# Scan stage of a vision-Mamba kernel on one core: dut tiles issued three products ahead, C rows before B rows, y stores in sub-slots 1 and 3, a third y buffer

## The chip, the core and the metric

The kernel runs on one core of one Trainium2 chip. The metric is the device time of one launch in microseconds (us). A core has five engines that run side by side, each with its own instruction stream: PE (TensorE, matrix products), DVE (VectorE), ACT (ScalarE), POOL (GpSimd) and SP (SyncE). SP computes nothing: here it issues every DMA, in the order of its stream. "HBM" is the chip's main memory; SBUF and PSUM are the core's own memories.

## What is computed

The reference takes x of shape 8 x 96 x 64 x 64 and runs two layers: a state-space block, then attention without softmax and a quantised feed-forward block. The part that matters here is the selective scan of the first layer. For each image, each of four directions k, each of 192 channels and each of 16 states, along L = 4096 positions:

```python
def step(h, t):
    u_t, d_t, B_t, C_t = t
    dA = jnp.exp(d_t[..., None] * A)
    h = dA * h + (d_t * u_t)[..., None] * B_t[:, :, None, :]
    y = jnp.einsum('bkdn,bkn->bkd', h, C_t)
    return (h, y)
```

So a decay factor dA, a driving term delta*u*B, a linear recurrence over time, and a sum over the 16 states weighted by C.

## The kernel before

Eight images are handled as four pairs. For each pair the kernel first prepares delta, delta*u, B and C in scratch buffers in HBM (`dl`, `du`, `bs`, `cs`), then calls `scan` (L442). The preparation of a pair overlaps the closing stages of the pair before; `scan` runs alone. All times of `scan` below come four times in a launch.

`scan` walks over 128 steps: four directions, and in each 32 chunks of TC = 128 positions. Directions 2 and 3 run backwards. A chunk is cut into four quarters r of six channel groups, and each quarter into two halves z. The step loop (L656) has eight sub-slots v = 0..7 in a step, and p = 8s + v counts them over the whole scan. The schedule is written out by hand (`manual_schedule`, L444): every engine executes its instructions in the order in which the loop emits them, and only semaphores let one engine wait for another.

What the loop emits, with the engine that does it:

- `decay(p + 2)` (L572): six PE products of `aw` and `dm` into one of three PSUM buffers `da`, then an exponential on ACT (L588). It is two sub-slots ahead of its use.
- `drive(p // 2 + 2)` (L545), in even sub-slots: the driving term of one quarter. ACT copies the state at the end of the chunk before into the start column (L560; POOL's memset L558 at a direction's start), and POOL multiplies `dut` (delta*u) by the B rows of `bc` into `dbu` (L563). `dbu` has three buffers. One such POOL instruction is called a product below, and products are numbered g = 4s + r.
- `run(p)` (L590): the recurrence, one DVE instruction (L599) on a half of a quarter. It reads `da` from PSUM and `dbu` from SBUF and writes `h`. Two runs use one product.
- `sums(s - 1, f)` (L604): the sum over states of the step before, small PE products of `h` and `cw` (L617), and twice in a step an ACT evacuation into the y buffer `yev` (L625), at f = 3 (sub-slot v = 2) and f = 7 (v = 6).
- `fetch(g)` (L529): SP's load of `dut[g]`, 384 KB, into one of five buffers. The load of tile g must wait until product g - 5 has read the same buffer. Before the change, sub-slot p emits `fetch(p // 2 + 4)` after `drive(p // 2 + 2)`, thus two products ahead.
- `load(s + 2, v // 2)` (L478), in odd sub-slots: two SP loads of `dm` (L489, L490), 144 and 48 KB, for the decay two steps later.
- `load_aw` (L470): the weights of the next direction, four loads of 384 KB, only in a direction's last step.
- `load_bc(s + 2)` (L492): B rows and C rows for two chunks (NB = 2), as four SP loads of 128 KB (L501), one after each of the sub-slots v = 0..3 of an even step. Before the change the two B loads come first, the two C loads second.
- `diagonal(s + 1)` (L509): from the C rows, the weights `cw` for the sums. It is spread over the eight sub-slots of an odd step; each has one ACT instruction (L517), which reads the C rows in `bc`, and one SP load of 16 KB (L523).
- `store(s - 2, j)` (L630): SP's store of one half of `yev`, 96 KB (L635). Before the change in v = 2 and v = 6, from one of two `yev` buffers.

The order on SP's stream within a sub-slot is thus: `fetch` or `load` (and `load_aw`), then `store`, then the one load of `load_bc` or `diagonal`. In two steps, one even and one odd, SP issues 8 dut, 16 dm, 4 bc, 8 cw and 4 y transfers, 40 in all.

Of the kernel before, what the change touches and what calls it, by code (L numbers as in the profile page):

```python
# [10 lines left out]
F32 = mybir.dt.float32  # L11
# [26 lines left out]
HQ = TC // 4  # L38
NE = 24
# [13 lines left out]
def vss_attn_ffn(ctx: ExitStack, tc: tile.TileContext, a: dict):  # L53
# [388 lines left out]
    def scan(dl, du, bs, cs_, ys):  # L442
        with ExitStack() as st:
# [4 lines left out]
            wk = st.enter_context(tc.tile_pool(name="s2", bufs=2))  # L448
            trio = st.enter_context(tc.tile_pool(name="s3", bufs=3))
# [18 lines left out]
            aw, dm, bc, dut, dbu, hs, yev = {}, {}, {}, {}, {}, {}, {}  # L468

            def load_aw(k, r):  # L470

                aw[k, r] = one.tile([128, NI, 2, 128], BF16, name=f"aw{r}")
                w = 2 * NI * 128
                nc.sync.dma_start(
                    aw[k, r].rearrange("p i z m -> p (i z m)"), awd[k, :, r * w : r * w + w]
                )
# [15 lines left out]
            def load_bc(s):  # L492

                if s >= N:
                    return
                k, c, _ = steps[s]
                i = s // NB
                bc[i] = wk.tile([128, 2, 2, NB * TC], F32, name="bc")
                for w, v in enumerate((bs, cs_)):
                    for b in range(2):  # L500
                        nc.sync.dma_start(  # L501
                            bc[i][64 * b : 64 * b + 64, w].rearrange("p z t -> p (z t)"),
                            v[k, c // NB, 16 * b : 16 * b + 16]
                            .rearrange("(n z) t -> n (z t)", z=2)
                            .unsqueeze(0).to_broadcast([8, 8, 2 * NB * TC]),
                        )
                        yield
# [21 lines left out]
            def fetch(g):  # L529

                if g >= 4 * N:
                    return
                k, c, _ = steps[g // 4]
                o = NI * (g % 4)
                dut[g] = quad.tile([128, NI, TC], F32, name="dut")
                nc.sync.dma_start(
                    dut[g].rearrange("p i t -> p (i t)"),
                    du[k, c, :, o : o + NI].rearrange("m i t -> m (i t)").unsqueeze(1)
                    .to_broadcast([16, 8, NI * TC]),
                )  # L540
# [4 lines left out]
            def drive(g):  # L545

                if g >= 4 * N:
                    return
                s, r = divmod(g, 4)
                k, c, first = steps[s]  # L550
                back = k >= 2
                t = trio.tile([128, 2 * W6 + 1], F32, name="dbu")
                if back:
                    start = t[:, 1:].rearrange("p (z i u) -> p z i u", z=2, u=SEG)[:, :, :, TC]
                else:
                    start = segs(t)[:, :, :, 0]
                if first:
                    nc.gpsimd.memset(start, 0.0)  # L558
                else:
                    nc.scalar.copy(  # L560
                        start, segs(hs[s - 1][:, :, r])[:, :, :, 1 if back else TC]
                    )
                nc.gpsimd.tensor_tensor(  # L563
                    segs(t)[:, :, :, 1:],
                    dut[g].unsqueeze(1)
                    .to_broadcast([128, 2, NI, TC]),
                    bc[s // NB][:, 0, :, bass.ts(c % NB, TC)].unsqueeze(2)
                    .to_broadcast([128, 2, NI, TC]), ALU.mult,
                )
                dbu[g] = t  # L570

            def decay(p):  # L572

                if p >= 8 * N:
                    return
                s, v = divmod(p, 8)
                r, z = divmod(v, 2)
                k, c, _ = steps[s]
                e = da[p % 3][:, 0:W6].rearrange("p (i u) -> p i u", u=SEG)[:, :, 1:]
                for i in range(NI):  # L580
                    nc.tensor.matmul(  # L581
                        e[:, i], aw[k, r][:, i, z, :], dm[s // 2][:, NI * r + i, bass.ts(c % 2, TC)],
                        start=True, stop=True,
                    )
                if p == 0:
                    table("ln", lambda: nc.scalar.activation(e, e, AF.Exp))
                else:
                    nc.scalar.activation(e, e, AF.Exp)  # L588

            def run(p):  # L590
                s, v = divmod(p, 8)
                r, z = divmod(v, 2)
                if v == 0:
                    hs[s] = wk.tile([128, 2 * W6 + 1, NR], F32, name="h")
                o = 1 if steps[s][0] >= 2 else 0
                d = slice(None, None, -1) if o else slice(None)

                w = slice(z * W6 + o, z * W6 + o + W6)
                nc.vector.tensor_tensor_scan(  # L599
                    hs[s][:, w, r][:, d], da[p % 3][:, o : o + W6][:, d],  # L600
                    dbu[4 * s + r][:, w][:, d], 0.0, ALU.mult, ALU.add,
                )

            def sums(s, f):  # L604


                c = steps[s][1]
                if f == 0:
                    yev[s] = wk.tile([128, 2, HQ // 2, NE], F32, name="yev")
                y = yp[f // 4]  # L610
                h = hs[s][:, 1:, :].rearrange("p (z i u) r -> p z i u r", z=2, u=SEG)
                w = cw[s // NB % 2][:, :, c % NB].rearrange("p z m (j t) -> p z (m j) t", j=2)
                for i in range(2 * (f % 4), 2 * (f % 4) + 2):
                    for z in range(2):
                        for q in range(4):
                            t = 16 * q + 8 * (f // 4) + i
                            nc.tensor.matmul(  # L617
                                y[32 * q : 32 * q + 32, 2 * NE * i : 2 * NE * i + 2 * NE]
                                .rearrange("p (j r i) -> p i j r", j=2, r=NR),
                                w[:, z, :, t], h[:, z, :, t : TC : TC // 2, :],  # L620
                                start=(i + z == 0), stop=(i + z == 8),
                            )
                if f % 4 == 3:
                    o = 8 * (f // 4)
                    nc.scalar.activation(  # L625
                        yev[s][:, :, o : o + 8, :].rearrange("p j i e -> p i j e"),
                        y[:, 0 : 16 * NE].rearrange("p (i j e) -> p i j e", j=2, e=NE), AF.Copy,
                    )

            def store(s, j):  # L630
                k, c, _ = steps[s]
                v = ys[k, :, c * TC : (c + 1) * TC, :].rearrange(
                    "m (j q i) e -> j q m (i e)", j=2, q=4
                )
                nc.sync.dma_start(v[j], yev[s][j::2, j].rearrange("p i e -> p (i e)"))  # L635
# [6 lines left out]
            for _ in load_bc(0):  # L642
                pass
# [4 lines left out]
                pass  # L648
            fetch(2)
            fetch(3)  # L650
            more = iter(())
            drive(0)
            drive(1)
# [2 lines left out]
            for s in range(N + 2):  # L656
                for v in range(8):
                    p = 8 * s + v
                    if s < N:
                        decay(p + 2)  # L660
                        if v % 2 == 0:
                            drive(p // 2 + 2)
                        run(p)
                    if 0 < s <= N:
                        for f in ((0, 1), (2,), (3,), (4,), (5,), (6,), (7,), ())[v]:
                            sums(s - 1, f)
                    if s < N:
                        if v % 2 == 0:
                            fetch(p // 2 + 4)
                        else:  # L670
                            load(s + 2, v // 2)
                        if s + 1 < N and steps[s + 1][2] and v % 2 == 1:
                            load_aw(steps[s + 1][0], v // 2)
                    if v in (2, 6) and s > 1:
                        store(s - 2, v // 4)
                    if v == 0:
                        more = diagonal(s + 1) if s % NB else load_bc(s + NB)
                    next(more, None)
# [216 lines left out]
    for pair in range(npair + 1):  # L895
# [60 lines left out]
        if new:  # L956
            scan(new["dl"], new["du"], new["bs"], new["cs"], new["ys"])
# [115 lines left out]
```

## Time and profile before

| what | us |
|---|---|
| median of three launches | 11598.43 (11579.95 to 11607.51) |
| the profiled execution: its time | 11616.03 |
| the profiled execution: its span, first to last instruction | 11613.8 |
| scan of pair 0, stretch 597 to 2500 of the span | 1903: DVE busy 1759.1, POOL 1774.2, ACT 1266.5, PE 1289.7 |
| the other three scans, stretches cut alike | 1911, 1900, 1904 |
| DMA engines in the scan of pair 0 | mean busy share 0.75, 198 GB/s |
| mean granted TensorE clock | 0.818 of full speed |

The profile is one execution with the hardware profiler on. Its page has the busy time of each engine, 40 equal slices of the span, the DMA queues, the chain of work that ended last, the costliest groups of instructions and the DMA issues. Further views of the trace list waits, instructions in order of time, and busy time in chosen stretches. "SPq" marks instructions of SP's sequencer. A row "A <- B: t, n, m" in the view of waits means that A's engine stood idle t us in total, n times, at most m us, until B released it. The program's page does not count DMA-issuing instructions as busy, so SP has no busy share there; its load has to be read from the timeline.

### The profile page before, as it was taken

How to read it: one execution, taken by the hardware profiler on the slowest of the kernel's cores; microseconds unless marked ns; L12 is line 12 of the kernel's file. 1: busy time of each engine (PE TensorE's matmuls, PEld its weight loads, DVE VectorE, ACT ScalarE, POOL GpSimd, SP SyncE). 2: the span in 40 equal slices, each digit the busy share in tenths (PEclk: the TensorE clock that was granted, in tenths of full speed). 3: DMA queues.
4: the chain of work that ended last, by engine and by line, in shares of the span. 5: the costliest groups of instructions: out<-in, count | busy, mean ns of one | idle time of the engine just before them, and what ended most of it. 6: DMA issues, size and time to landing. Idle time of an engine off the chain costs nothing. (4 is left out here: it accounts for less than half of the span.)

```text
span 11613.8 us, 392166 instructions
## 1 busy us (share of the span) xinstructions
PE 8533.6 (73%) x170112; PEld 5690.3 (49%) x170112; DVE 8826.8 (76%) x6465; ACT 6941.0 (60%) x12227; POOL 7976.2 (69%) x2770
## 2 busy tenths in 40 slices
PE   7866666679876666667996666666898666666687
PEld 2255555544325555554422555555442355555542
DVE  5489999963659999995366999999445799999922
ACT  3666666644556666664455666666446566666623
POOL 0489999960259999994026999999203799999900
PEclk8778878889768787888977888888896787888886
DMA  2977777765477777776557777777636877777762
GB/s 83 234 196 203 199 201 201 200 169 137 131 198 198 200 197 202 204 200 157 123 150 204 198 202 198 201 205 198 150 98 180 206 199 201 202 199 202 194 137 62
DMA packets 1755459, 2096.48 MB, mean 181 GB/s; under 512 B 438019, under 2 KB 1340676, under 8 KB 1750916
## 3 DMA queue, kind: packets, MB, share of 16 engines
q1 hardware_dynamic: 1753732, 2071.39, 68.3%
q8 instruction: 1335, 21.87, 0.8%
q14 instruction: 392, 3.21, 0.1%
HBM read 1606.70 MB, written 464.01 MB: 178 GB/s over the span
## 5 line engine op out<-in xcount | busy, mean ns | idle before, releaser
L599 DVE TENSOR_TENSOR_SCAN h<-da,dbu 128x774 f32<-128x774 f32 x4096 | 7034.7, 1759 | 599.7 <-POOL dbu L563 450.3
L563 POOL TENSOR_TENSOR dbu<-dut,bc 128x1536 f32<-128x1536 f32 x2048 | 7092.1, 3509 | 546.5 <-DMA dut<-du 334.2
L581 PE MATMUL da<-dm,aw 128*128 128x128 bf16 x24576 | 2488.2, 250 | 2523.7 <-DVE h L599 2313.4
L588 ACT ACTIVATE da<-da 128x768 f32<-128x768 f32 x4092 | 3255.0, 796 | 1583.2 <-PE da L581 1572.2
L581 PEld LDWEIGHTS <-aw 128*128 128x128 bf16 x24576 | 1943.3, 111 | 2809.5 <-issue 2444.5
L617 PE MATMUL yp<-h,cw 128*32 128x48 f32 x131072 | 2995.4, 246 | 38.7 <-issue 25.3
L617 PEld LDWEIGHTS yp<-h,cw 128*32 128x32 f32 x131072 | 2475.2, 155 | 526.3 <-issue 257.2
L517 ACT ACTIVATE cw<-bc,blk 128x512 f32<-128x512 f32 x2048 | 1462.9, 716 | 574.8 <-DMA bc<-cs 492.6
L757 POOL TENSOR_TENSOR yk<-yk 128x768 f32<-128x768 f32 x64 | 116.5, 1820 | 1267.3 <-DMA yk<-ys 1095.3
L433 POOL TENSOR_TENSOR dp<-rest,dp 128x512 bf16<-128x512 f32 x384 | 473.8, 1237 | 680.6 <-ACT dp L432 678.8
L625 ACT ACTIVATE yev<-yp 128x384 f32<-128x384 f32 x1024 | 504.1, 492 | 466.5 <-DMA ys<-yev 336.0
L431 DVE TENSOR_TENSOR rest<-delta,dp 128x512 f32<-128x512 f32 x384 | 335.3, 876 | 426.9 <-ACT dp L430 426.6
L410 PE MATMUL pq<-S,dtw 12*128 12x512 f32 x768 | 555.5, 833 | 111.8 <-ACT delta L414 95.7
L798 DVE SCALAR_TENSOR_TENSOR g<-yc,c_onw,yrs 96x512 f32<-96x512 f32 x128 | 89.9, 742 | 473.3 <-ACT yrs L190 473.3
L870 POOL TENSOR_TENSOR ot<-t,y 96x512 f32<-96x512 f32 x64 | 101.8, 1591 | 487.8 <-DVE y L868 395.6
L560 ACT COPY dbu<-h 128x12 f32<-128x12 f32 x1984 | 404.0, 204 | 0.0
L432 ACT ACTIVATE dp<-rest 128x512 bf16<-128x512 f32 x384 | 240.1, 628 | 272.5 <-DVE rest L431 272.1
L410 PEld LDWEIGHTS pq<-S,dtw 12*128 12x128 f32 x768 | 154.6, 236 | 497.2 <-ACT delta L414 262.0
L684 ACT ACTIVATE nsq<-ncp 96x512 f32<-96x512 f32 x128 | 75.8, 592 | 533.2 <-PE ncp L682 506.5
L390 POOL COPY u<-xi 128x512 f32<-128x512 f32 x96 | 100.6, 1063 | 347.4 <-ACT xi L356 293.5
L770 PEld LDWEIGHTS py<-ident,yk 128*24 128x24 f32 x8192 | 228.2, 106 | 225.0 <-issue 169.1
L770 PE MATMUL py<-ident,yk 128*24 128x128 f32 x8192 | 310.2, 285 | 26.7 <-DVE yk L756 22.7
(136 smaller groups left out, 6783.5 us busy)
## 6 DMA issues: line engine op xcount, KB each, us to landing
dut<-du SPq DMA_DIRECT2D x2048, 384.0 KB
dm<-dl SPq DMA_DIRECT2D x2048, 144.0 KB
dl<-dp SPq DMA_DIRECT2D x256, 384.0 KB
dm<-dl SPq DMA_DIRECT2D x2048, 48.0 KB
ys<-yev SPq DMA_DIRECT2D x1024, 96.0 KB
du<-du SPq DMA_DIRECT2D x256, 256.0 KB
bc<-bs SPq DMA_DIRECT2D x512, 128.0 KB
bc<-cs SPq DMA_DIRECT2D x512, 128.0 KB
```

The costliest lines, as they stand in the source:

```text
L410: nc.tensor.matmul(pq, dtw[64:76, k, T], S[64:76], start=True, stop=True)
L431: nc.vector.tensor_tensor(rest, d, dp[:, :, 0], ALU.subtract)
L433: nc.gpsimd.tensor_tensor(dp[:, :, 2], rest, dp[:, :, 1], ALU.subtract)
L517: nc.scalar.activation(cw[i % 2][:, :, :, m, :].rearrange("p z j t -> p (z j) t"), bc[i][:, 1].rearrange("p z (j t) -> p (z j) t", j=NB), ...
L560: nc.scalar.copy(start, segs(hs[s - 1][:, :, r])[:, :, :, 1 if back else TC])
L563: nc.gpsimd.tensor_tensor(segs(t)[:, :, :, 1:], dut[g].unsqueeze(1) .to_broadcast([128, 2, NI, TC]), bc[s // NB][:, 0, :, bass.ts(c % NB, ...
L581: nc.tensor.matmul(e[:, i], aw[k, r][:, i, z, :], dm[s // 2][:, NI * r + i, bass.ts(c % 2, TC)], start=True, stop=True,)
L588: nc.scalar.activation(e, e, AF.Exp)
L599: nc.vector.tensor_tensor_scan(hs[s][:, w, r][:, d], da[p % 3][:, o : o + W6][:, d], dbu[4 * s + r][:, w][:, d], 0.0, ALU.mult, ALU.add,)
L617: nc.tensor.matmul(y[32 * q : 32 * q + 32, 2 * NE * i : 2 * NE * i + 2 * NE] .rearrange("p (j r i) -> p i j r", j=2, r=NR), w[:, z, :, t], ...
L625: nc.scalar.activation(yev[s][:, :, o : o + 8, :].rearrange("p j i e -> p i j e"), y[:, 0 : 16 * NE].rearrange("p (i j e) -> p i j e", j=2 ...
L770: nc.tensor.matmul(o, yk[:, k, 4 * g + e, NE * j : NE * j + NE], ident, start=False, stop=(k + j == 4),)
```

## The change

Four edits, all inside `scan`:

1. `load_bc` issues the two C loads first and the two B loads second.
2. `yev` moves from the pool with two buffers to the pool with three (one more tile of 3 KB in each partition).
3. `fetch(4)` is issued before the loop, and even sub-slots issue `fetch(p // 2 + 5)` in place of `fetch(p // 2 + 4)`. The tile then goes out three products ahead of the product that the same sub-slot emits. The number of `dut` buffers stays five.
4. The two stores of step s - 2 go out in sub-slots v = 0 and v = 2 of step s (the first and the third) in place of v = 2 and v = 6.

PE, DVE, ACT and POOL keep their instructions and their order. Only the order of SP's stream changes, and which buffers are shared.

```diff
@@ load_bc
-                for w, v in enumerate((bs, cs_)):
+                for w, v in ((1, cs_), (0, bs)):
                     for b in range(2):
                         nc.sync.dma_start(
@@ sums
                 if f == 0:
-                    yev[s] = wk.tile([128, 2, HQ // 2, NE], F32, name="yev")
+                    yev[s] = trio.tile([128, 2, HQ // 2, NE], F32, name="yev")
@@ before the loop
             fetch(2)
             fetch(3)
+            fetch(4)
@@ the loop
                         if v % 2 == 0:
-                            fetch(p // 2 + 4)
+                            fetch(p // 2 + 5)
                         else:
                             load(s + 2, v // 2)
...
-                    if v in (2, 6) and s > 1:
-                        store(s - 2, v // 4)
+                    if v in (0, 2) and s > 1:
+                        store(s - 2, v // 2)
```

In SP's stream of an even and an odd step, numbered from the even step's first `fetch`, the stores stand at places 6, 15, 24 and 35 before the change and at 1, 7, 19 and 25 after it; the C loads at 7 and 10 before and at 2 and 5 after; the B loads at 1 and 4 before and at 8 and 11 after.

## The prediction

> **What bounds the kernel now.** I read the page's costliest groups first. Each group line gives line, engine, operation and shapes, then busy us and mean ns, then idle us before it and what ended most of that idle.
>
> ```profile
> L599 DVE TENSOR_TENSOR_SCAN h<-da,dbu 128x774 f32<-128x774 f32 x4096 | 7034.7, 1759 | 599.7 <-POOL dbu L563 450.3
> L563 POOL TENSOR_TENSOR dbu<-dut,bc 128x1536 f32<-128x1536 f32 x2048 | 7092.1, 3509 | 546.5 <-DMA dut<-du 334.2
> ...
> L517 ACT ACTIVATE cw<-bc,blk 128x512 f32<-128x512 f32 x2048 | 1462.9, 716 | 574.8 <-DMA bc<-cs 492.6
> ...
> L625 ACT ACTIVATE yev<-yp 128x384 f32<-128x384 f32 x1024 | 504.1, 492 | 466.5 <-DMA ys<-yev 336.0
> ```
>
> The four scans are the long stages. DVE waits for POOL's product, POOL waits for dut, and ACT waits for C rows and for y stores. These are the waits that the four edits aim at. But a wait for a DMA can mean "issued too late in the order" or "the queue cannot go faster". So I read POOL's timeline next (start, length; 8 products are two chunks):
>
> ```profile
> 1306.66 27.70 POOL L563 TENSOR_TENSOR dbu<-dut,bc 128x1536 f32<-128x1536 f32 x8 [2.08 <-DMA dut<-du]
> 1335.95 27.71 POOL L563 TENSOR_TENSOR dbu<-dut,bc 128x1536 f32<-128x1536 f32 x8 [1.59 <-DMA dut<-du]
> ```
>
> POOL runs eight products without a gap in 27.70 us, then loses about 1.8 us, once in two chunks. Two chunks are also SP's cycle: one even chunk with four bc loads, one odd chunk with eight cw loads, 40 issues in all. The SP timeline from the end of an even chunk's first half:
>
> ```profile
> 1327.84 0.58 SPq L501 DMA_DIRECT2D bc<-cs  x1
> 1328.53 0.54 SPq L536 DMA_DIRECT2D dut<-du  x1
> 1329.48 0.58 SPq L489 DMA_DIRECT2D dm<-dl  x1
> 1330.69 0.31 SPq L490 DMA_DIRECT2D dm<-dl  x1
> 1331.69 0.52 SPq L536 DMA_DIRECT2D dut<-du  x1
> 1332.69 0.59 SPq L635 DMA_DIRECT2D ys<-yev  x1
> ...
> 1338.24 0.70 SPq L523 DMA_DIRECT2D cw<-cs  x1
> 1339.05 0.56 SPq L536 DMA_DIRECT2D dut<-du  x1
> 1339.70 0.64 SPq L635 DMA_DIRECT2D ys<-yev  x1
> 1340.39 0.68 SPq L523 DMA_DIRECT2D cw<-cs  x1
> ```
>
> SP issues back to back, 0.55 to 0.70 us each, except in a few holes around 1329 to 1333. The queue's own waits over the run say what those holes are:
>
> ```profile
> SPq L523 <- DMA dut<-du: 194.5, 273, 1.7
> SPq L635 <- DMA bc<-cs: 114.8, 197, 1.4
> SPq L490 <- DMA dut<-du: 104.5, 184, 1.5
> ```
>
> A cw load does not need a dut tile. In the built program each SP issue waits for the landing of the issue eight places before it (eight completion semaphores in turn), so at most eight transfers are in flight. Averaged over the steady part of the four scans, SP's cycle of 40 issues is 29.64 us: 24.65 in issues, 2.15 in hand-overs of 0.05 to 0.10 us, 2.69 waiting for the landing eight back, 0.16 other. The cycles without weight loads take 29.47. So SP is never idle for want of work, and it never waits for POOL: a dut issue stands 7 to 9 us after the product that freed its buffer. An early cycle of the first scan settles it: POOL still had a lead and took 27.68 us, while SP took 29.55. SP sets the pace; the others queue behind it.
>
> **What the Trainium skill says.** "DMA: Bandwidth & Descriptors", section "Why a DMA increments its semaphore by 16 and not by 1": a transfer uses the largest count of engines up to 16 that divides the slowest dimension of both sides, on this path the lowest-numbered ones, and the sequencer posts the rest of the count at once. The landing records agree: 16 engine landings for a dut or dm load, one early record and eight landings for a bc or cw load, one and four for a y store. So engines 0 to 3 carry everything, and 8 to 15 only dut and dm. Section "Queues, rings and completion order" of that page: an engine takes descriptors in ring order. This agrees: a y store issued after a dut in the crowded stretch lands 5.8 us after its issue, in a quiet stretch 4.1. "Perfetto Trace Analysis", section "DMA Instruction — HWDGE (DVE, Sync)": an issue's row ends when the sequencer is free, not when data landed; here the rows are 0.54 us and a dut lands 4.2 to 7.1 us after issue. "SBUF — State Buffer", section "Who interferes with whom": a DVE instruction with one SBUF input does not contend with GpSimd. The scan's other input is in PSUM, and 16 scans and 8 products lie side by side in 27.7 us each, so I price no collision.
>
> **The change part by part.** Number SP's issues in a cycle from 0, the even chunk's first dut.
>
> *Look-ahead of three.* No issue is added in the cycle; dut 4 goes out before the loop. Each dut stands 3.46 us (one product) earlier in the order, moved past one dm pair, one or two bc or cw loads and at times a store, which each go out one place (0.65 us) later and have slack of 8 slots and more. Its wait for product g-5 stays met: 7 to 9 us of slack minus 3.46 is over 3.5. This removes POOL's stall as seen against SP's order, but not SP's 29.47 us, so POOL's wait comes back later in the run. What remains is the end of each scan: the last dut stands one product nearer to the scan's first, worth up to 3.46 x 4 = 14 us, at least 0. I take 10.
>
> *C before B.* The same four bc transfers of 128 KB trade places: 0 on SP. ACT's wait for C (492.6/256 = 1.9 us a cycle) shrinks, but ACT is off the path: DVE waits little for it. B then lands about 13 us into the cycle, and its first reader runs at about 17 even with compute one product earlier, so this has cover. At a scan's start B lands some 3 us later and delays product 0, which the wait for the third dut (product 2 starts 20 us after the first issue) hides: 0.
>
> *Third y buffer.* ACT's 336.0 us wait for y stores goes. ACT has slack; nothing on SP: 0. If ACT were on the path, it would be worth up to 336.
>
> *Stores in sub-slots 1 and 3.* A store needs an evacuation two slots back, long done. All four stores stay, but stand at issues 1, 7, 19, 25 instead of 6, 15, 24, 35. This moves the landings that SP waits for, and is the only edit that can move SP's cycle. Averages of the trace: SP waits only from issue 12 to 24. The wait that decides is the one of issue 23, at 17.79 us, for the landing of issue 15, at 17.44. Issues 0 to 15 are the same sixteen transfers in both orders (4 dut, 4 bc, 2 y, 3 pairs of dm). If engines 0 to 3 work without a pause, that landing does not move. Today they pause early: issues 1, 2, 3 land 0.91, 0.82 and 0.48 us apart, against 1.1, 0.55 and 0.29 later for bc and the two dm, so the dm gaps hold about 0.5 us of idle. A store at issue 1 fills this: gain 0 to 0.5, I take 0.3. After issue 23 seventeen issues remain in both, with one store (0.66) less and one cw (0.73) more: +0.07. Stores at 19 and 25 make issue 27 wait for landing 19. Reckoned from the landing steps (dm 0.55 and 0.25, dut 1.1, y 0.77), landing 19 comes 0.45 us before issue 27 is due, so only the scatter of cycles (28.36 to 30.77 us, 5th to 95th percentile) makes it wait: 0 to 0.5, I take 0.1. Sum -0.3 + 0.07 + 0.1 = -0.13 us a cycle, bounds -0.43 to +0.57. Over 256 cycles: -33 us, bounds -110 to +146.
>
> Sum: -33 - 10 = -43 us against the profiled execution's 11616.03, so 11573. That execution is 17.6 above the median of 11598.43, so **11555**.
>
> **Rivals.** (1) *The order is the fault, not the queue.* With all waits gone POOL would run 27.70 a cycle: 256 x (29.47 - 27.70) = 453 us less, about 11145. For it: POOL's 334.2 us on dut, ACT's 828.6. Against: SP's 24.65 + 2.15 + 2.85, of which only the 2.85 can go. (2) *Nothing moves.* The landings of the same bytes decide, and all is within 0.2%: about 11590. (3) *Slower: the stores crowd engines 0 to 3.* A store right behind the dut at the start of both chunks, beside C or cw loads, and an even second half of only dut and dm, where eight issues hold more bytes. If this keeps SP waiting past issue 27, each y landing (0.77) that falls into the binding stretch counts: at +0.4 a cycle 102 - 10 = +92, so 11690. It decides the sign once SP's waits rise by over 0.04 us a cycle (10/256).
>
> **How the numbers follow.** A measurement of this kernel can tell about 0.2% (23 us) from no change. Chances: the small gain 0.45, around 11555, own range 11430 to 11575; rival 1 0.08; rival 2 0.19; rival 3 0.28. Faster 0.45 + 0.08 = 0.53, same 0.19, slower 0.28. The range goes from 11420 (bounds -110 - 14 and the scatter of runs, some 50) to 11720 (rival 3 near the upper bound); it leaves out rival 1 and a tenth for the slow end.
>
> **What would show it.** Right: SP's issues still back to back at about 27 us a cycle, its holes 2.4 to 2.9 us, the cycle 29.2 to 29.5; ACT's waits for C and y stores mostly gone, and POOL's idle total nearly as before. Step wrong if landing 15 does not come earlier than 17.44, or if SP's holes last beyond issue 27. Wrong altogether if the cycle falls towards 27.7, since then compute or the order paced SP, or if SP begins to wait for POOL at a dut issue.

## The result, and the profile after

The changed kernel takes **11560.52 us**, the median of eight launches (11552.50 to 11584.88). Eight launches of the kernel before, in turn with them, have a median of 11597.08 us. The ratio is 0.9973, with a 95% interval of 0.9962 to 0.9983: 20 to 44 us less, about 31. The forecast was 11555. In a second comparison (run 8 below) the same kernel took 11596.14 against 11618.52 us, ratio 0.9982 (0.9975 to 0.9989): 13 to 29 us less. So it is faster by a little, and whether by 20 or by 30 us is not settled. A ratio is taken over executions in the usual state and is not the quotient of the two medians; one execution of run 1 (13590.88 us) and one of run 3 (22200.87) were in a slow state and count in the medians alone.

The profiled execution took 11560.57 us, its span is 11558.7. From the first dut issue to the last recurrence the four scans took 1908.5, 1911.5, 1900.5 and 1904.4 us before and 1898.7, 1897.7, 1900.6 and 1897.3 after: 7625.0 to 7594.3, 30.7 us less. A second profile of the changed kernel (run 8) has 7615.4, only 9.6 less, so single profiles scatter by as much as the gain itself. The span fell by 55.1. The other 24 us of the first profile lie outside the scans, where no instruction differs; over all profiles of this study that remainder ran from 3947 to 3990 us, and the profiled execution of before, 3989, was near its top. So the two spans alone overstate the gain.

The costliest groups of the profile after, the same four as were shown of before (busy us, mean ns, then idle us before and what ended most of it):

```profile
L599 DVE TENSOR_TENSOR_SCAN h<-da,dbu 128x774 f32<-128x774 f32 x4096 | 7026.4, 1759 | 576.5 <-POOL dbu L563 328.6
L563 POOL TENSOR_TENSOR dbu<-dut,bc 128x1536 f32<-128x1536 f32 x2048 | 7090.9, 3505 | 516.2 <-DMA dut<-du 154.1
...
L517 ACT ACTIVATE cw<-bc,blk 128x512 f32<-128x512 f32 x2048 | 1469.5, 719 | 83.4 <-DMA bc<-cs 59.8
...
L625 ACT ACTIVATE yev<-yp 128x384 f32<-128x384 f32 x1024 | 504.6, 493 | 41.4 <-PE yp L617 40.6
```

All three waits at which the edits aim are smaller: POOL on dut 334.2 to 154.1, ACT on C rows 492.6 to 59.8, and ACT's 336.0 on y stores is gone. Yet the idle totals of the two engines that carry the recurrence have hardly moved: DVE 599.7 to 576.5, POOL 546.5 to 516.2. The waits have changed their names, not their sum. The view of waits, first before, then after, says where they went:

```profile
PE da L581 <- DMA dm<-dl: 117.8, 36, 30.6
```

```profile
PE da L581 <- DMA dm<-dl: 546.5, 251, 29.9
...
POOL dbu L563 <- DMA dut<-du: 154.1, 121, 4.7
...
POOL dbu L563 <- ACT dbu L560: 147.1, 99, 5.3
...
POOL dbu L563 <- DMA dm<-dl: 135.3, 63, 19.4
```

PE's wait for dm was 117.8 us (36 times) before and is 546.5 (251 times) now. That is SP's queue again: dm goes out of the same queue as dut. PE's timeline after shows how such a wait looks: three of the six matrix products of one decay run, and the other three wait until their part of dm has landed (start, length, count, idle time before):

```profile
1313.84 0.33 PE L581 MATMUL da<-dm,aw 128*128 128x128 bf16 x3 [0.54 <-DVE h L599]
1314.97 0.34 PE L581 MATMUL da<-dm,aw 128*128 128x128 bf16 x3 [0.80 <-DMA dm<-dl]
```

POOL's timeline in the same steady stretch shows the loss under another name:

```profile
1289.54 38.04 POOL L563 TENSOR_TENSOR dbu<-dut,bc 128x1536 f32<-128x1536 f32 x11 [1.86 <-ACT dbu L560]
1329.10 44.91 POOL L563 TENSOR_TENSOR dbu<-dut,bc 128x1536 f32<-128x1536 f32 x13 [1.52 <-ACT dbu L560]
1375.30 10.44 POOL L563 TENSOR_TENSOR dbu<-dut,bc 128x1536 f32<-128x1536 f32 x3 [1.29 <-ACT dbu L560]
```

Before, each gap was ended by dut. Now it is ended by ACT's start column (L560), which needs the end of the recurrence, which needs the decay, which needs dm. The SP timeline after, issues 15 to 20 of a cycle in the prediction's numbering, still has its holes:

```profile
1323.73 0.52 SPq L536 DMA_DIRECT2D dut<-du  x1
1325.01 0.56 SPq L489 DMA_DIRECT2D dm<-dl  x1
1325.81 0.38 SPq L490 DMA_DIRECT2D dm<-dl  x1
1326.30 0.51 SPq L536 DMA_DIRECT2D dut<-du  x1
1327.40 0.59 SPq L635 DMA_DIRECT2D ys<-yev  x1
1329.01 0.72 SPq L523 DMA_DIRECT2D cw<-cs  x1
```

And the queue's waits after name a wait at a cw issue for a dut tile that cw does not use, as before, so the wait is for the landing eight issues back:

```profile
SPq L523 <- DMA dut<-du: 237.2, 348, 2.0
```

The averages of SP's cycle of 40 issues over the steady part of the four scans, worked out from the traces as for the prediction (us; with the cycles that load weights). "In issues" is the sum of the issue rows, "hand-overs" the short gaps between rows, "landing eight back" the waits for that landing:

| kernel | cycle | in issues | hand-overs | landing eight back | other |
|---|---|---|---|---|---|
| before | 29.64 | 24.65 | 2.15 | 2.69 | 0.16 |
| after | 29.50 | 24.98 | 2.21 | 2.15 | 0.16 |
| after, second profile | 29.61 | 25.02 | 2.19 | 2.23 | 0.17 |

One profile's cycle scatters by about 0.1 us. So the fall in the waits for the landing eight back is real (it is there twice), some two thirds of it come back in the issue rows themselves, and the cycle's own change is too small to be read from one profile.

### The profile page after: what moved, and what is told of

It is laid out like the page before. It is cut to its first block, busy times and chain, and to the rows that moved or that the text cites. A ratio compares the mean times of both kernels' runs of the same rounds, so it can differ in the third digit from the quotient of the medians.

```text
span 11558.7 us, 392143 instructions
## 1 busy us (share of the span) xinstructions
PE 8468.6 (73%) x170112; PEld 5607.4 (49%) x170112; DVE 8817.7 (76%) x6465; ACT 6982.1 (60%) x12227; POOL 7973.4 (69%) x2770
## 5 line engine op out<-in xcount | busy, mean ns | idle before, releaser
L599 DVE TENSOR_TENSOR_SCAN h<-da,dbu 128x774 f32<-128x774 f32 x4096 | 7026.4, 1759 | 576.5 <-POOL dbu L563 328.6
L563 POOL TENSOR_TENSOR dbu<-dut,bc 128x1536 f32<-128x1536 f32 x2048 | 7090.9, 3505 | 516.2 <-DMA dut<-du 154.1
L581 PEld LDWEIGHTS <-aw 128*128 128x128 bf16 x24576 | 1882.9, 110 | 2870.1 <-issue 1999.4
L517 ACT ACTIVATE cw<-bc,blk 128x512 f32<-128x512 f32 x2048 | 1469.5, 719 | 83.4 <-DMA bc<-cs 59.8
L560 ACT COPY dbu<-h 128x12 f32<-128x12 f32 x1984 | 410.7, 207 | 0.0
L410 PEld LDWEIGHTS pq<-S,dtw 12*128 12x128 f32 x768 | 154.1, 235 | 494.8 <-ACT delta L414 263.5
```

The costliest lines, as they stand in the source:

```text
L410: nc.tensor.matmul(pq, dtw[64:76, k, T], S[64:76], start=True, stop=True)
L517: nc.scalar.activation(cw[i % 2][:, :, :, m, :].rearrange("p z j t -> p (z j) t"), bc[i][:, 1].rearrange("p z (j t) -> p (z j) t", j=NB), ...
L560: nc.scalar.copy(start, segs(hs[s - 1][:, :, r])[:, :, :, 1 if back else TC])
L563: nc.gpsimd.tensor_tensor(segs(t)[:, :, :, 1:], dut[g].unsqueeze(1) .to_broadcast([128, 2, NI, TC]), bc[s // NB][:, 0, :, bass.ts(c % NB, ...
L581: nc.tensor.matmul(e[:, i], aw[k, r][:, i, z, :], dm[s // 2][:, NI * r + i, bass.ts(c % 2, TC)], start=True, stop=True,)
L599: nc.vector.tensor_tensor_scan(hs[s][:, w, r][:, d], da[p % 3][:, o : o + W6][:, d], dbu[4 * s + r][:, w][:, d], 0.0, ALU.mult, ALU.add,)
```

## The experiments

The theory is the prediction's: **SP's stream of 40 issues, with at most eight in flight, sets the pace**, and the order of the stream matters only where it moves a landing that SP waits for. The rival is that the order was the fault, and that POOL or ACT waited for loads that came too late in it.

**1. Look-ahead of three alone**, on the kernel before:

```diff
+            fetch(4)
...
-                            fetch(p // 2 + 4)
+                            fetch(p // 2 + 5)
```

> The kernel before with the look-ahead edit alone (dut 4 before the loop, tile p//2+5 in each even sub-slot). Queue theory (SP's stream of 40 issues and the landing eight places back set the pace): the stream has the same issues and almost the same neighbours, so no gain in the cycle: -15 to +15 us of 11597, ratio 0.999 to 1.001; POOL's wait for dut shrinks but another wait takes its place (the dm tiles for PE). Rival (dut was issued too late in the order): most of POOL's 334 us goes, at least 150 us faster, ratio under 0.987.

Measured: 11612.0 against 11616.0 us, ratio 0.9991 (0.9983 to 0.9999). The groups of its profile, and PE's row for dm from its view of waits:

```profile
L563 POOL TENSOR_TENSOR dbu<-dut,bc 128x1536 f32<-128x1536 f32 x2048 | 7097.2, 3511 | 523.6 <-ACT dbu L560 380.1
...
L517 ACT ACTIVATE cw<-bc,blk 128x512 f32<-128x512 f32 x2048 | 1462.4, 715 | 743.9 <-DMA bc<-cs 647.1
...
PE da L581 <- DMA dm<-dl: 121.1, 46, 30.5
```

POOL's wait for dut fell from 334.2 to 37.9 us, nearly all of it, and POOL's idle total went only from 546.5 to 523.6: 380.1 now wait for the start column. The wait that took its place is not the one that was expected: PE's wait for dm stayed (117.8 to 121.1), and ACT's wait for C rows, which stands ahead of the next start columns in ACT's stream, grew from 492.6 to 647.1 and is the likelier cause. A wait was removed and the time stayed. The rival falls for this edit.

**2. The stores alone:**

```diff
-                    if v in (2, 6) and s > 1:
-                        store(s - 2, v // 4)
+                    if v in (0, 2) and s > 1:
+                        store(s - 2, v // 2)
```

> The kernel before with the y stores moved to sub-slots v = 0 and v = 2, two y buffers, nothing else. Queue theory: this is the only edit that shifts the landings that SP waits for; it carries the whole gain, about -0.13 us a cycle, -33 us (-10 to -60), ratio 0.995 to 0.999. Rival (the stores move nothing, the gain is in look-ahead or C rows): within 10 us.

Measured: 11601.58 against 11616.0, ratio 0.9991 (0.9984 to 0.9997), so 3 to 19 us less. The direction was as forecast; the term of 33 us was too large, and the interval does not tell the gain from the rival's "within 10 us". In the trace the landing of issue 15 comes 17.41 us into the cycle (17.44 before), issue 23 at 17.59 (17.79). So that landing hardly moved; issue 23 came earlier because it follows the landing more closely.

**3. C rows first and the third y buffer alone:**

```diff
-                for w, v in enumerate((bs, cs_)):
+                for w, v in ((1, cs_), (0, bs)):
...
-                    yev[s] = wk.tile([128, 2, HQ // 2, NE], F32, name="yev")
+                    yev[s] = trio.tile([128, 2, HQ // 2, NE], F32, name="yev")
```

> The kernel before with C rows before B rows and the third y buffer, nothing else. Queue theory: ACT's waits for C rows and y stores (492.6 and 336.0 us) mostly go, the time stays: -15 to +15 us, ratio 0.999 to 1.001. Rival (ACT's waits are on the path): at least 100 us faster.

Measured: 11614.13 against 11616.0, ratio 0.9997 (0.9989 to 1.0006). Its groups:

```profile
L563 POOL TENSOR_TENSOR dbu<-dut,bc 128x1536 f32<-128x1536 f32 x2048 | 7091.0, 3507 | 555.2 <-DMA dut<-du 380.5
...
L517 ACT ACTIVATE cw<-bc,blk 128x512 f32<-128x512 f32 x2048 | 1467.2, 718 | 68.8 <-DMA bc<-cs 68.8
...
L625 ACT ACTIVATE yev<-yp 128x384 f32<-128x384 f32 x1024 | 505.1, 493 | 63.3 <-PE yp L617 62.4
```

The idle time ahead of these two ACT lines fell from 1041.3 us (574.8 and 466.5) to 132.1, and the launch is as long as before. ACT now spends that time waiting for PE's matrix products of the decay (1572.2 before, 2438.4 here). ACT waited because it had time.

**4. Two useless loads in a cycle**, on the changed kernel: SP reads 12 KB that nobody uses into a spare tile, once in every step. It adds work to the queue, hardly any bytes, and no work to an engine that computes:

```diff
+            spare = one.tile([32, 96], F32, name="spare")
...
+                    if v == 6 and s < N:
+                        nc.sync.dma_start(spare, a["gmat"][0:32, 0:96])
```

> The changed kernel with one useless load of 12 KB more in each step, at v = 6, into a spare tile that nobody reads: two more issues of about 0.65 us in SP's cycle of two steps, no more work for any other engine. Queue theory: the one in the odd step adds its full 0.65 us, the one in the even step falls where SP waits for landings and may hide: 256 x 0.65 to 256 x 1.3 = 170 to 330 us slower than the changed kernel, ratio to before 1.011 to 1.026. Rival (compute or data rate sets the pace, SP has slack of 1.8 us a cycle): within 25 us of the changed kernel, ratio 0.995 to 0.999.

Measured: 11928.88 against 11616.0, ratio 1.0270 (1.0257 to 1.0283). Beside the changed kernel's two ratios that is 335 to 345 us, or 1.3 us a cycle for two issues: each adds its whole row and hand-over, none is hidden. SP's cycle rose from 29.50 to 30.96, its issue rows from 24.98 to 26.23. If SP had slack, this would have cost nothing. The cost is even a little above what was expected.

**5. Half as many dm loads**, on the changed kernel: the same bytes in 288 and 96 KB in place of 144 and 48 KB, twice in a step in place of four times. SP has 32 issues in a cycle in place of 40:

```diff
-                w = NE // 8
-                o = 4 * w * (s % 2) + w * part
+                w = NE // 4
+                o = 2 * w * (s % 2) + w * part
...
-            for j in range(4):
+            for j in range(2):
...
-                        else:
-                            load(s + 2, v // 2)
+                        elif v % 4 == 1:
+                            load(s + 2, v // 4)
```

(The loop of `range(4)` stands twice ahead of the step loop; both are changed.)

> The changed kernel with the dm loads of two neighbouring parts merged (two pairs a step at v = 1 and v = 5, 288 and 96 KB, instead of four pairs of 144 and 48 KB): the same bytes, eight issues fewer in SP's cycle of 40. Queue theory: 8 x 0.63 = 5.0 us of issue time go, SP's own load falls from 27 to 22 us, and the cycle falls until the next bound holds it: POOL's 27.70 us, or engines 0 to 3 [...]and eight in flight that now hold more bytes: 27.7 to 28.5 us a cycle, 250 to 450 us faster than the changed kernel, ratio to before 0.958 to 0.976. Rival (bytes in flight or landing times, not issues, set the pace): within 50 us of the changed kernel, ratio over 0.993.

Measured: **11140.51 against 11623.44 us, ratio 0.9585 (0.9572 to 0.9598)**. POOL's group, and its timeline in about the same stretch of the launch:

```profile
L563 POOL TENSOR_TENSOR dbu<-dut,bc 128x1536 f32<-128x1536 f32 x2048 | 7082.8, 3571 | 92.6 <-DMA dut<-du 45.8
...
1228.54 242.10 POOL L563 TENSOR_TENSOR dbu<-dut,bc 128x1536 f32<-128x1536 f32 x70
```

Seventy products without a gap, 3.46 us each, 27.7 for eight; POOL's idle time ahead of its products fell from 516.2 to 92.6 us. And SP's queue for the first time waits for compute:

```profile
SPq L536 <- POOL dbu L563: 832.3, 671, 2.9
```

Reckoned from the trace, 751 of the 2048 dut issues start within 0.3 us of the end of the product whose buffer they need. Before the figure is 2, after it is 0. The pace has passed from SP to POOL. Each scan takes 1793 to 1796 us. Beside the changed kernel's two ratios the gain is some 450 to 460 us, at the upper end of the 250 to 450 that were expected.

Two other causes of this gain can be weighed by the traces. The merge also makes the transfers' pieces longer: by the DMA records, a cycle moves the same 5.94 MB in some 2710 packets in place of 3350. But the 16 DMA engines were busy 22.7 to 22.9 us a cycle on average in run 5 and 22.1 to 22.3 in the changed kernel, so it was not their work that shrank (the average does not single out engines 0 to 3). And the mean granted TensorE clock was 0.87 here, 0.83 in the changed kernel and 0.81 in run 4: it went up as the cycle got shorter. What moves it was not tested. The other engines' instructions did not get shorter with it (the recurrence took 1759 ns before and here, the exponential 796 and 797), and PE spent most of its idle time before the decay waiting for the recurrence (2313.4 us before, 2065.8 here), so the time is not put down to the clock.

**6. The same on the kernel before** (edit of 5 without the four edits of the change).

> The same merge of dm loads on the kernel before, without the four edits. Queue theory: with SP's load gone, the order of issue matters at last: dut two ahead, C rows second and two y buffers make compute wait, so it is slower than the merge on the changed kernel by some 50 to 200 us, but faster than before by 100 to 350 us, ratio 0.970 to 0.991. Rival (the edits are worth nothing in any setting): equal to the merge on the changed kernel within 0.2%.

Measured: 11190.62 against 11623.44, ratio 0.9621 (0.9608 to 0.9635). That is faster than expected, and the changed kernel's four edits are now worth 50 us more. SP's cycle is 27.94 us: issues 19.51 (5.1 less than before), but 6.49 waiting for the landing eight back (2.69 before). The cycle fell by less than the rows, since POOL's 27.7 us are its floor (run 5); SP, which now has the time, waits for landings instead, and stays 0.2 us a cycle above that floor.

**7 and 8. Look-ahead and stores together, and the whole change again**, to see whether the parts add and whether C rows and y buffer give anything.

```diff
+            fetch(4)
...
-                            fetch(p // 2 + 4)
+                            fetch(p // 2 + 5)
...
-                    if v in (2, 6) and s > 1:
-                        store(s - 2, v // 4)
+                    if v in (0, 2) and s > 1:
+                        store(s - 2, v // 2)
```

> Look-ahead and stores together on the kernel before, B rows still first, two y buffers. If the small gains simply add (0.9991 and 0.9991 alone): 0.998, and the whole change some 0.0003 more. If the C rows matter once the dut is early (ACT waited 647 us for C rows with the look-ahead alone): this one stays at 0.9985 to 0.999 and the whole change is clearly faster, 0.9965 to 0.998.

Run 8 is the changed kernel without any edit.

> The whole change once more, on the same chip as the part of it: 0.9962 to 0.9983 as in its first measurement. It tells whether the parts add up to the whole.

Measured: 11586.75 (ratio 0.9976, 0.9967 to 0.9985) and 11596.14 (0.9982, 0.9975 to 0.9989) against 11618.52. Within the noise the two parts add up to the whole (-10, -10, together -28, the whole -21, with intervals of some 8 to 10 us either way). The other two edits add nothing that can be seen.

**9, 10 and 11. Which part is worth the 50 us once dm is merged?** Each has the edit of 5 on the kernel before, and one part of the change: the edit of run 1, of run 3, of run 2.

```diff
+            fetch(4)
...
-                            fetch(p // 2 + 4)
-                        else:
-                            load(s + 2, v // 2)
+                            fetch(p // 2 + 5)
+                        elif v % 4 == 1:
+                            load(s + 2, v // 4)
```

> The merge of dm loads on the kernel before, with the look-ahead edit alone (B rows first, two y buffers, stores as before). With SP's queue free, theory: the look-ahead is the edit that counts, since dut is what POOL waits for: within 15 us of the merge on the whole change, ratio 0.957 to 0.960. Rival: C rows and y buffers count as much, then it lies half way, 0.960 to 0.962.

Measured: 11194.52 against 11618.52, ratio 0.9638 (0.9625 to 0.9650). The look-ahead gives nothing here either (0.9621 without it, on another chip). The idea that it pays as soon as the queue has room fell. What it did is move SP's waiting, as SP's queue shows:

```profile
SPq L536 <- POOL dbu L563: 645.7, 673, 2.9
```

Reckoned as in the table above, SP waits 3.9 us a cycle for the landing eight back in place of run 6's 6.49, and 2.9 at dut issues for POOL; the cycle, 27.96 us, is no shorter.

```diff
-                for w, v in enumerate((bs, cs_)):
+                for w, v in ((1, cs_), (0, bs)):
...
-                    yev[s] = wk.tile([128, 2, HQ // 2, NE], F32, name="yev")
+                    yev[s] = trio.tile([128, 2, HQ // 2, NE], F32, name="yev")
```

> The merge of dm loads on the kernel before with C rows first and the third y buffer, no look-ahead, stores as before. With SP's queue free, the look-ahead gave nothing there, so what is left of the gap between 0.962 and 0.9585 must come from ACT's waits or from the stores. Theory (ACT's waits now reach POOL and DVE): most of the gap, ratio 0.957 to 0.960. Rival (stores, or only the edits together): 0.961 to 0.964.

Measured: 11187.93 against 11605.84, ratio 0.9636 (0.9621 to 0.9651). Nothing. That ACT's waits would begin to count fell too.

```diff
-                    if v in (2, 6) and s > 1:
-                        store(s - 2, v // 4)
+                    if v in (0, 2) and s > 1:
+                        store(s - 2, v // 2)
```

> The merge of dm loads on the kernel before with the stores at v = 0 and v = 2 alone. Theory (ACT's waits hold the merged kernel back): a store that lands earlier frees the y buffer earlier, so a part of the gap only, ratio 0.960 to 0.963. Rival (it is the landings that SP waits for, 6.5 us a cycle in the merged kernel): 0.957 to 0.960.

Measured: **11139.17 against 11605.84, ratio 0.9598 (0.9584 to 0.9613)**: as fast as run 5 with all four edits. SP's waits for the landing eight back fell from 6.49 us a cycle (run 6) to 2.46, the cycle from 27.94 to 27.75, and POOL runs without a gap, in the same stretch of the launch:

```profile
1229.14 242.04 POOL L563 TENSOR_TENSOR dbu<-dut,bc 128x1536 f32<-128x1536 f32 x70
```

The cycle's 0.19 us times 256 are 49 us, as large as the step from run 10, taken on the same chip (11187.93 to 11139.17). The rest of the saved waiting turns into waiting for compute: 2.10 at dut issues for POOL and 1.81 at stores for ACT's evacuation. The rival of this run's expectation held as to the time. So the place of the stores is the one edit of the four with a use once dm is merged. That it works through the landings is likely, but not shown: in run 9 the waits for landings fell as well, by 2.6 us a cycle, and no time was gained.

## Why the prediction was right

**What bounds the kernel: right, and shown.** Two issues more cost 1.3 us a cycle (run 4), eight fewer took POOL's idle time from 516.2 to 92.6 us (run 5), and the three edits that removed other waits (runs 1 and 3) moved 10 us or nothing. The page's lines `<-DMA dut` and `<-DMA bc` were true as to what ended the wait, and misleading as to what to mend. The Trainium skill, "Perfetto Trace Analysis", section 'What "DMA-bound" means', lists an issuing sequencer whose track is solid with DMA slices as one of the things that a DMA-bound kernel can be bound on. The trace agrees, 27.2 of 29.5 us in issues and hand-overs after, with one addition: where SP's track is not solid, it waits mostly for the landing eight back, 2.69 us a cycle before, 2.15 after and 6.49 in run 6.

**C before B 0, third y buffer 0: right** (runs 3 and 10; run 8 beside run 7).

**Look-ahead, 10 us: right in size, not in its place** (run 1: 1 to 20 less). The prediction put it at the ends of the scans. The four scans of run 1 are 9 and 13 us shorter and 1 and 4 us longer than before, and the ends show no gain: from the first dut issue to the loop's first cw issue, and from the last dm issue to the last recurrence, a scan takes 56.6 us before, 57.2 in run 1, and 55.7 and 55.3 in the two profiles of the changed kernel. So the whole change may have gained 1 us a scan there, the look-ahead alone nothing, and that the size came out is in part luck.

Two statements on the way were wrong. The passed dm loads do not have "slack of 8 slots and more": the pair issued in v = 7 of an odd step holds the last elements (21 to 23) of the tile for the next two chunks, which the decay emitted in v = 4 of the next step reads. That is five sub-slots later in the order, some 8.6 us at 3.46 us for two. In the traces the decay emitted beside a cycle's first fetch starts 4.2 us ahead of that fetch before and 7.1 us after, which leaves about 1.5 us for a landing that takes 3.2 to 3.7 in the median. Hence PE's 546.5 us. It takes more than the look-ahead: in run 1, where ACT waited 647.1 us for C rows, that lead grew to only 4.8 us, and PE's wait for dm was 121.1; with the stores it was 277.6 (run 7), with C rows first as well 546.5 and 564.4 (run 8). And the slack of a dut issue behind the product that frees its buffer did not fall by 3.46 in the changed kernel: its medians by place in the cycle were 7.1 to 8.7 before and are 5.7 to 8.3 after, never under 2.7 in the steady part, because compute moved ahead of SP by nearly as much. In run 1, where it did not, they are 4.5 to 6.2. None of this cost time, since SP sets the pace whichever of its loads is late last; for the same reason "POOL's wait comes back later in the run" held.

**Stores, 33 us: the sign right, the size too large, the mechanism borne out in part** (run 2: 3 to 19; in the unmerged kernel the part's share of the whole stays blurred, since both parts measure 10 with overlapping intervals). The terms of its sum:

| term, us a cycle | forecast | after and its second profile |
|---|---|---|
| landing of issue 15 | -0.3 | -0.14, -0.10 (17.44 to 17.30, 17.34) |
| issue 23, which waits for it | -0.3 | -0.32, -0.26 (17.79 to 17.47, 17.53) |
| the seventeen issues after it | +0.07 + 0.1 | +0.23, +0.26 (11.68 to 11.91, 11.94) |
| sum | -0.13 | -0.09, 0.00 |

The landing moved by less than half of what was reckoned from the idle gap between the early dm landings, and with the stores alone by 0.03 us only (run 2), less than profiles differ by; that a store fills the gap is thus not shown. Issue 23 moved by about the forecast amount all the same, since it now follows the landing by 0.17 to 0.19 us where it was 0.35. The tail cost more than forecast. The stores at 19 and 25 lie near the stretch where SP waits, and rows of over 0.85 us come 1.87 times a cycle, 1.46 before, so part of the waiting may now sit inside the issue rows. That would be the rival of the crowded engines 0 to 3 in small; it took back a part, not the sign. The second profile's sum is 0.00, so these terms do not carry the measured gain on their own.

**The forecast of 11555 came out 5.5 us from the measured median**, which is luck, since its terms were not that close: with the measured 10 for each part the same sum gives 11578 by the first median of before.

**What would show it.** SP still back to back, the cycle without weight loads 29.38 (29.2 to 29.5 was named), ACT's waits gone, POOL's total nearly as before, the landing of issue 15 ahead of 17.44: all so. SP's holes were to be 2.4 to 2.9 and are 2.15, while the issue rows grew by 0.33. The page's view after still has 145.1 us of SP waiting for POOL at a dut issue (94.4 before), but in the steady part no dut issue starts within 2.7 us of that product's end (1.2 in the first steps of a scan): the label names the latest of the semaphores waited for that the profile knows of, not what held the issue.

**The rivals.** "The order is the fault" gave 11145 and was wrong for this change. Its price for a scan paced by compute, 453 us, was near what the relieved queue gave (run 5: 482 us less than the kernel before in the same comparison). "Nothing moves" (11590) is nearest after the forecast; the second comparison's interval (13 to 29 us) does not tell it from a gain just over 0.2%. The slower rival fell.

**Left open:** whether the gain is 20 or 30 us, how much of it is outside the scans, by what way the stores gain, and whether stores that use all 16 DMA engines would help the holes, which was not tried. The mean granted TensorE clock was 0.83 in the executions of the changed kernel and 0.81 to 0.82 in those of the kernel before; run 7, without the C and y edits, had 0.81 to 0.82 too and was not slower than run 8, so no time of the change can be put down to it.

## What to carry to other kernels

When an engine waits for a DMA, look at the issuing queue before its order: if issues stand back to back, or stop only for the landing a fixed number of places back, then moving loads may only rename the waits, and fewer issues are worth a try. Here merging eight of 40 issues into their neighbours was worth 3.8% where the four edits together were worth 0.2 to 0.3%. A cheap test is to add one useless small transfer per cycle: if the run grows by the whole issue row, the queue is the bound. Issuing a part of the loads from another engine, the other way to relieve the queue, was not tried.

## What the runs showed of the hardware

- A DMA issue on SP's queue cost about the same for dm loads of different size: median rows of 0.597 us for 288 KB and 0.579 for 96 KB of dm in run 5, 0.59 for 144 KB before. With the hand-over an issue cost some 0.65 us: two more of 12 KB took 1.3 us a cycle.
- The issue row is not a constant. Some rows were longer than 0.85 us, 1.46 a cycle before and 1.87 after, most of them 0.9 to 1.7 us; what stretches them is not shown. The second dm row (L490) was as short as 0.31 to 0.38 us right after a hole, as at 1325.81 above.
- A fifth of the issues less did not shorten the cycle by their rows: in run 6, 5.1 us of rows and 0.7 of hand-overs less gave 1.7 us of cycle, since POOL's products take 27.7 us and SP's waits for landings rose by 3.8 and others by 0.3.
